# Two expert blocks of layer 0 moved into layer 1's opening list, a fourth early block in layer 1, and other PSUM banks for the first transposes

## The chip, the cores and the metric

The kernel runs on one core of a Trainium2 chip. The metric is the device time of one launch in microseconds (us). Before the change it is 1606.35 us, the median of three runs that lie between 1605.81 and 1606.99. The page of the profile shows one execution with a span of 1586.5 us, taken by the hardware profiler; the rest of a launch lies outside the span. In the page PE is TensorE's matmul, PEld its weight load, DVE is VectorE, ACT is ScalarE, POOL is GpSimd, and SP is SyncE, which here only starts transfers.

## The reference, cut to what matters

The input is x with N = 2708 rows of C = 256 floats, and an adjacency matrix of 2708 x 2708. Two layers follow each other. Each adds two terms to x:

```python
# layer 0
x = x + gnn0(layernorm(x), adj)      # softmax(leaky_relu(f1 + f2.T) + adj) @ h
x = x + ffn0(layernorm(x))           # causal attention with 4 heads, then 8 experts, 2 per row
# layer 1
x = x + gnn1(layernorm(x), adj)      # sigmoid(softmax(leaky_relu, masked by (adj != 0) | eye) @ Xp)
x = x + ffn1(layernorm(x))           # 8 experts, 2 per row, no attention
# the experts of a layer, flat = its normalised rows
for e in range(8):                   # weights: zero for all but the row's two best experts
    out += weights[:, e:e+1] * ((silu(flat @ w1[e].T) * (flat @ w3[e].T)) @ w2[e].T)
```

An expert's hidden width is 682. All matmuls that matter here are in float32. A row of layer 1's input x1 is complete only when both of its experts in layer 0 have added their share, and layer 1's graph attention mixes all rows.

## The kernel before

The 2708 rows are cut into NT = 22 tiles of 128 (the last holds 20). The kernel has four stages, and each is a stretch of the profile.

**`first`** is layer 0 up to its routing: the graph attention, the causal attention, and `route`, which picks two experts for each row and sends the row, with its gates and its index, by an indirect transfer (L1769) into the list of each of its experts in the DRAM buffer `xs[0]`. An expert's list is cut into NB = 6 blocks of 128 places, so a layer has 48 blocks. Within a list the rows stand in the order of their tiles. As soon as enough tiles have been sent (the `EARLY` numbers 12, 12, 18), the first three blocks of expert 0 are computed inside the same stage, by `early_blocks` (L514 to L582).

**`experts_blocks(0)`** is a plain loop over the other 45 blocks. For each it fetches the block's rows (`fetch`, `xt<-xs`), transposes them with two matmuls (L274) and copies them back on ACT (L276, L279), does 22 matmuls with w1 and w3 (`up`, L1981), the silu on ACT (L1985, L1988), the gate product on DVE (L1986, L1989), 6 matmuls with w2 (`down`, L1995), the row's weight on DVE (L1997) and an indirect scatter-add on POOL into `acc` in DRAM (`add_rows`, L598). Each float32 matmul shows as two records in the profile. Transposes and copies run ahead of the block that uses them. Three rooms hold the weights of three experts; `arena` is two of them, and expert 7's weights are in its second half, `arena[:, WE:]`.

**`second`** is layer 1 up to its routing. It loads x1, which is `acc`, from DRAM into `X` with five transfers (L1486, L1489). `prepare` makes of every tile its features: statistics on DVE (L257, L259, L1436), a power on POOL (L1440), the scaling on DVE (L1444), two transposes on PE (L1450) into a PSUM bank, a copy back on ACT (L1454), the matmuls with the layer's weights (L1459, L1462), and the results to `hb` and `sb` by DVE and ACT (L1466 to L1472). The 22 target tiles are taken in groups of six (four groups, the last with four tiles). For a group the mask of the adjacency, which `first` left in DRAM as bf16 (`mb`), is brought in by transposing transfers (L1504); for each source tile ACT makes the exponentials (L1511), DVE turns the mask to zeros and ones (L1516, L1520) and multiplies (L1522), and PE adds six products into six PSUM banks (L1529). Group 0's masks lie in `arena`, where layer 0's weights were, group 1's in a buffer of their own, and so on in turn. When a group is through, `finish` (L1575 to L1588) joins it to x, and `route` sends its rows into `xs[1]`. Three early blocks of expert 0 end this stage too.

**`experts_blocks(1)`** is the same loop over 45 blocks, with `out` in the place of `acc`.

The order within `first` and `second` is not written out by hand. `Plan` is a list scheduler that runs while the program is built. A step has an engine, a planned length, the steps it needs, the buffers it takes and gives back, a rank, and `lands`, the time until its transfer has landed. `issue` always takes the step that could start soonest in its planned time, the smaller rank first among those that can start together, and so fixes the order in which each engine meets its instructions. Every engine then works strictly in that order. Where the plan sees PE idle for over 1 us, `fill` puts matmuls named `nobody` there (L1248, L1630), whose results are not used; `issue(behind=5.0)` does so once more at the end of the list.

PSUM has eight banks. `second` uses six of them under the name `po` (the sums of a group, or the `up` results of an early block) and two under the name `mm` for everything else.

A flag is raised on the device if a block holds rows that its early place does not allow; if it is set, the whole network is computed again in a general form.

Of the kernel before, what the change touches and what calls it, by code (L numbers as in the profile page):

```python
# [39 lines left out]
EARLY = 12, 12, 18  # L40

CAP = (NT + 1) * P
# [99 lines left out]
def adj_ffn_kernel(ctx, tc, x, adj, vecs, bias_rows, tab, w_gnn0, w_gnn1, wqkv, wo,  # L142
# [216 lines left out]
    def route(add, tiles, ready, copied, cleared, layer, XB, xs, pool, turn_tile, turn_bank, gate_tile, gate_bank, rank):  # L359
# [151 lines left out]
        return [add("POOL", 2.3, lambda t=t: send(t), [b, c] + cleared, rank=rank + 6, lands=2.0) for t in tiles]  # L511


    def early_blocks(add, layer, needs, sent, we, xs, acc, new, named, rank):  # L514

        for k, before_t in enumerate(EARLY):
            v = {}
            names = dict(named, up=named["up"][k % len(named["up"])], xt=named["xt"][k % len(named["xt"])])

            def fetch(k=k, v=v):  # L520
                v["xt"] = new["xt"](k)
                after_all(nc.sync.dma_start(out=v["xt"], in_=xs[k * P:(k + 1) * P, :]), xs)
# [16 lines left out]
            def up(part, k=k, v=v):  # L539
# [28 lines left out]
            def down(half, v=v):  # L568
# [5 lines left out]
            def weigh(v=v):  # L574
                v["ys"] = new["ys"]()
                nc.vector.tensor_scalar(v["ys"], v["y"][:, :C], v["xt"][:, C + 1:C + 2], None, ALU.mult)
# [5 lines left out]
            a = add("SP", 0.4, fetch, (needs if layer == 0 else []) + sum([sent[t] for t in sent if t < before_t], []), take=[names["xt"]], rank=r, lands=3.0)  # L582
# [11 lines left out]
            add("POOL", 1.6, join, [a], give=[names["ys"], names["xt"]], rank=r)  # L594
# [174 lines left out]
    def first(X, XB, norms, tops, hd, mb, xs, acc, arena, load_weights):  # L769
# [11 lines left out]
        with ExitStack() as s:  # L781
# [449 lines left out]
            def chunks():  # L1231
# [4 lines left out]
                         weights_at(arena[:, :WE]), xs[0], acc,  # L1236
                         dict(xt=lambda k: (ab.tile([P, 2 * W2], F32, tag="osb", name="xt") if k == 2 else
                                            af.tile([P, NQK], F32, tag=("qk", "z")[k], name="xt"))[:, :ROW],
                              mm=mm_tile, xT=lambda: af.tile([P, KC, P], F32, tag="hT", name="xTs", bufs=3),
                              up=up_banks, sl=chunks, hT=chunks,  # L1240
                              ys=lambda: af.tile([P, C], F32, tag="xg", name="ys", bufs=3)),
                         dict(xt=["qk", "z", "ob"], mm="mm", xT="hT", up=[["st", "zs"], ["st", "o"], ["st", "o"]], sl="e", hT="e", ys="xg"), 60.0)
# [9 lines left out]
            with tc.manual_schedule():  # L1252
                plan.issue(behind=5.0)
# [143 lines left out]
    def second(X, XB, x1, x2, sd, mb, xs, arena, load_weights):  # L1397
# [9 lines left out]
        with ExitStack() as s:  # L1407
# [86 lines left out]
            def aggregate(g, tiles):  # L1494
# [72 lines left out]
                for i in tiles:  # L1567
                    finish(i, v, done, rank + NT + 2 + 3 * (i - tiles[0]), ["z"] * (i == tiles[-1]))
# [610 lines left out]
```

## Time and profile before

The table gives stretches of the profiled execution in us from the start of the span: their length, how long PE was busy in them (with the unused matmuls `nobody`), and the clock that was granted to TensorE.

| stretch | what runs there | length | PE busy | clock |
|---|---|---|---|---|
| whole span | | 1586.5 | 1483.3 | 0.97 |
| 600–700 | inside the loop of layer 0 | 100.0 | 100.0 | 1.00 |
| 525–531 | end of `first`, last early block | 6.0 | 6.0 | |
| 531–537 | `nobody`, then the loop's first transposes | 6.0 | 5.5 | |
| 885–891 | last block's end, then `nobody` | 6.0 | 5.8 | 1.00 |
| 891–899 | x1 is loaded | 8.0 | 0.0 | 0.62 |
| 899–906 | first tiles prepared | 7.0 | 5.7 | 0.70 |
| 906–916 | more tiles prepared | 10.0 | 8.9 | |
| 916–922.3 | wait for the first mask | 6.3 | 2.8 | |
| 922.3–963 | first group's products between the other tiles | 40.7 | 40.7 | 0.96 |
| 1183–1194 | after the last product: results joined, rows sent | 10.6 | 10.6 | |
| 1194–1203 | routing, early blocks | 9.0 | 6.8 | |
| 1203–1214 | early blocks | 11.0 | 11.0 | |
| 1214–1222.5 | `nobody`, then the loop's first rows | 8.5 | 6.0 | |

To read it: PE is busy for 93% of the span, DVE for 47%, ACT for 35% and POOL for 31%. Inside the expert loops PE has no gap. The stretches that are not full, or are full of `nobody`, lie at the seams between the four stages. A busy share counts `nobody` as work, so a seam is judged by what stands in it, not by its share.

### The profile page before, as it was taken

The numbers are of one execution on the slowest core, as the hardware profiler recorded it, in microseconds if no ns is written. First come the engines' busy times: TensorE is split into PE (matmuls) and PEld (weight loads), VectorE is DVE, ScalarE is ACT, GpSimd is POOL, SyncE is SP. The second block draws the span as 40 slices with busy tenths as digits, with TensorE's granted clock in tenths as the row PEclk, the third lists the DMA queues.
The fourth block names the chain that finished last, engine by engine and source line by source line (L and its number), as shares of the span: only waits on it lengthen the run. The fifth ranks groups of instructions, "written<-read, shape, count | busy, mean of one in ns | idle before, by whom it ended". The sixth has DMA issues, their size and how long they took to land. (4 is left out here: it accounts for less than half of the span.)

```text
span 1586.5 us, 23363 instructions
## 1 busy us (share of the span) xinstructions
PE 1483.3 (93%) x8998; PEld 1155.8 (73%) x8998; DVE 745.5 (47%) x1477; ACT 553.6 (35%) x1065; POOL 487.9 (31%) x680
## 2 busy tenths in 40 slices
PE   6888889889989999999999789999998999999996
PEld 5633433323335999999999678888768999999995
DVE  6798899955666122221111464766664221112221
ACT  3676676555544112111111263444332111111110
POOL 6665457462142222222211210030425122222121
PEclk9999899999999999999999899999999999999998
DMA  7688565440012233333222670524414333323111
GB/s 254 237 294 301 190 221 193 154 156 7 7 49 78 55 77 91 88 88 76 47 38 32 145 155 1 130 70 99 132 49 121 77 86 86 74 66 74 33 33 17
DMA packets 165998, 165.69 MB, mean 104 GB/s; under 512 B 81378, under 2 KB 145550, under 8 KB 163168
## 3 DMA queue, kind: packets, MB, share of 16 engines
q1 hardware_dynamic: 142582, 134.26, 28.0%
q0 software_dynamic: 19024, 26.24, 9.1%
q10 hardware_dynamic: 4270, 3.58, 0.7%
q8 instruction: 73, 1.20, 0.3%
q14 instruction: 49, 0.40, 0.1%
HBM read 87.38 MB, written 61.55 MB: 94 GB/s over the span
## 5 line engine op out<-in xcount | busy, mean ns | idle before, releaser
L1981 PEld LDWEIGHTS pup<-xTs,arena 128*128 128x128 f32 (+1 forms) x2904 | 332.9, 190 | 3.9 <-ACT xTs L279 0.7
L1981 PE MATMUL pup<-xTs,arena 128*128 128x128 f32 (+1 forms) x2904 | 335.0, 275 | 0.5 <-ACT xTs L279 0.5
L1986 DVE TENSOR_TENSOR hT<-sl,pup 128x640 f32<-128x640 f32 x90 | 73.9, 821 | 478.6 <-ACT sl L1985 478.6
L1985 ACT ACTIVATE sl<-pup 128x640 f32<-128x640 f32 x90 | 63.4, 704 | 520.3 <-PE pup L1981 510.1
L1529 PE MATMUL po<-hb,PT 128*128 128x257 f32 (+1 forms) x968 | 226.7, 388 | 2.9 <-DVE PT L1522 2.9
L1529 PEld LDWEIGHTS po<-hb,PT 128*128 128x128 f32 (+1 forms) x968 | 175.6, 188 | 43.1 <-issue 12.5
L1995 PE MATMUL y<-arena,hT 128*128 128x256 f32 x792 | 182.1, 380 | 0.6 <-DVE ys L1997 0.6
L1088 ACT ACTIVATE e<-stt 128x1024 f32<-128x1024 f32 (+1 forms) x132 | 126.6, 986 | 98.9 <-PE stt L1082 73.9
L1995 PEld LDWEIGHTS y<-arena,hT 128*128 128x128 f32 x792 | 145.3, 190 | 18.0 <-DVE ys L1997 1.0
L598 POOL DMA_INDIRECT acc<-ys,xt x48 | 74.9, 1559 | 247.1 <-DVE ys L1997 238.6
L598 POOL DMA_INDIRECT out<-ys,xt x48 | 74.7, 1557 | 245.0 <-DVE ys L1997 238.1
L1127 DVE TENSOR_TENSOR es<-es,e 128x1024 f32<-128x1024 f32 x104 | 125.8, 1210 | 38.4 <-ACT e L1088 31.7
L1082 PE MATMUL stt<-qT,kT 64*128 64x512 f32 (+1 forms) x528 | 134.3, 615 | 6.7 <-ACT e L1088 6.7
L1769 POOL DMA_INDIRECT xs<-XR,place x88 | 92.0, 1046 | 145.1 <-DVE mk L1516 40.2
L1108 PE MATMUL o<-e,V 128*64 128x512 f32 (+1 forms) x528 | 130.6, 618 | 1.6 <-ACT e L1088 1.2
L1981 PEld LDWEIGHTS pup<-xTs,room 128*128 128x128 f32 (+1 forms) x1056 | 121.2, 190 | 1.2
L1981 PE MATMUL pup<-xTs,room 128*128 128x128 f32 (+1 forms) x1056 | 121.9, 275 | 0.0
L1511 ACT ACTIVATE E<-sb,dcol 128x768 f32<-128x768 f32 (+1 forms) x88 | 75.2, 859 | 105.3 <-DVE PT L1522 105.0
L1082 PEld LDWEIGHTS stt<-qT,kT 64*128 64x128 f32 x528 | 44.1, 188 | 79.3 <-issue 61.0
L1108 PEld LDWEIGHTS o<-e,V 128*64 128x64 f32 x528 | 33.6, 141 | 77.0 <-issue 58.2
L1997 DVE TENSOR_SCALAR ys<-y,xt 128x256 f32<-128x256 f32 x90 | 43.5, 484 | 55.4 <-PE y L1995 55.4
L1995 PE MATMUL y<-room,hT 128*128 128x256 f32 x288 | 66.1, 379 | 0.0
(273 smaller groups left out, 1814.0 us busy)
## 6 DMA issues: line engine op xcount, KB each, us to landing
arena<-in_adj SPq DMA_DIRECT2D x21, 1354.0 KB, 7.5
arena<-in_w SPq DMA_DIRECT2D x36, 640.0 KB, 4.6
mb<-mb SPq DMA_DIRECT2D x44, 352.0 KB, 3.6
xs<-none SPq DMA_DIRECT2D x16, 804.0 KB, 8.0
xt<-xs SPq DMA_DIRECT2D x96, 134.0 KB, 2.1
room<-in_w SPq DMA_DIRECT2D x12, 640.0 KB, 4.5
acc<-X SPq DMA_DIRECT2D x21, 128.0 KB, 3.7
out<-X SPq DMA_DIRECT2D x21, 128.0 KB, 1.8
```

What stands on the lines that cost most here:

```text
L598: nc.gpsimd.indirect_dma_start(out=acc[:, :], out_offset=bass.IndirectOffsetOnAxis(ap=xt[:, C:C + 1].bitcast(I32), axis=0), in_=ys, in_off ...
L1082: nc.tensor.matmul(st[:r, g, c0(sb):], kT[a:b, sb * P:sb * P + r], qT[a:b, t0 + (sb == t0 + 1):t0 + 2, :, :], start=True, stop=True)
L1088: nc.scalar.activation(e[:r, :, c0(sb):], v[sb, "st"][:r, :, c0(sb):], AF.Exp, scale=1.0 / HD ** 0.5)
L1108: nc.tensor.matmul(v["o"][g * HD:(g + 1) * HD, c:], V[:r, sb, g * HD:(g + 1) * HD], v[sb][:r, g, c:], start=(n + i == 0), stop=(n + i == t ...
L1127: nc.vector.tensor_tensor(es, es, v[sb][:r, :, c:], ALU.add)
L1511: nc.scalar.activation(e[:q, :n], sb[:q, i0:i1], AF.Exp, bias=dcol[:q, j:j + 1], scale=SLOPE - 1.0)
L1529: nc.tensor.matmul(v["po", i][:r, :F], v["PT", j][:q, a:a + r], hb[:q, j, :], start=(j == 0), stop=(j == NT - 1))
L1769: i = nc.gpsimd.indirect_dma_start(out=xs[:, :], out_offset=bass.IndirectOffsetOnAxis(ap=at, axis=0), in_=src, in_offset=None)
L1981: nc.tensor.matmul(pp[:to, n, :], wn[:, c, :], xT[:, c, :], start=(c == 0), stop=(c == KC - 1))
L1985: nc.scalar.activation(sl, pp[:, :NF, :], AF.Silu)
L1986: nc.vector.tensor_tensor(hT[:, :NF, :], sl, pp[:, NF:2 * NF, :], ALU.mult)
L1995: nc.tensor.matmul(y, hT[:, n, :], w[3][:, n, :], start=(n == 0), stop=(n == NHC - 1))
```

## The change

The change works on the three seams.

- **Late blocks.** The last two blocks of layer 0, (7,4) and (7,5), leave the loop and become steps of `second`'s list (`LATE`). The tiles 0 to 11 of x1 are loaded before them, the tiles 12 to 21 after both have added their rows: a block this far back in its list holds rows of tiles from 12 on only, so the first load doesn't need it. `some_blocks` is the old `early_blocks`, made general to serve both; the blocks' rows are fetched into slots of `XR`, whose index column is written anew by an `iota` on POOL after the late blocks. Expert 7's weights are in the second half of `arena`, where the second half of group 0's masks will be. So these masks are now kept by tile (`by_tile`), three tiles of them are transposed in before the late blocks and three after, and the mask operations of group 0 take the new layout through rearranged views.
- **A fourth early block.** In layer 1 the block (1,0) is computed inside `second` as well, so that its loop has 44 blocks. The checks of the early and late blocks move to later places in the loops (`missed`, one flag for each block).
- **Other banks.** The first eight tiles' transposes of `prepare` take `po` banks, which are free until the first product, and leave the two `mm` banks to the matmuls behind them.
- **Planner.** `issue()` no longer puts matmuls at the list's end; planned lengths and lands are set anew (a send 2.7 instead of 2.3, a transpose 0.3, a product 0.44), and in the third group the joins stand 1 instead of 3 apart and routing begins at rank 8 instead of 14.

The aim is to have needed matmuls where PE now waits or does unused ones.

```diff
-EARLY = 12, 12, 18
+EARLY = ((0, 0, 12), (0, 1, 12), (0, 2, 18)), ((0, 0, 12), (0, 1, 12), (0, 2, 18), (1, 0, 12))
+LATE, LATE_T = ((7, 4), (7, 5)), 12
...
-        return [add("POOL", 2.3, lambda t=t: send(t), [b, c] + cleared, rank=rank + 6, lands=2.0) for t in tiles]
+        return [add("POOL", 2.7, lambda t=t: send(t), [b, c] + cleared, rank=rank + 6, lands=2.0) for t in tiles]
...
-    def early_blocks(add, layer, needs, sent, we, xs, acc, new, named, rank):
-        for k, before_t in enumerate(EARLY):
+    def some_blocks(add, layer, blocks, fetched, needs, weights, xs, acc, new, named, rank):
+        joins = []
+        for k, (e, j, before) in enumerate(blocks):
+            v = dict(xt=fetched[k])
+            we = weights(e)
...
+        return some_blocks(add, layer, blocks, [XR[:, k, :] for k in range(len(blocks))], needs, *rest)
...
-                plan.issue(behind=5.0)
+                plan.issue()
...
+                bank = "po" if t < 8 else "mm"
...
-                    v["pt"] = pt = psm.tile([P, 4, P], F32, tag="mm", name="pt")
+                    v["pt"] = pt = (pso if bank == "po" else psm).tile([P, 4, P], F32, tag=bank, name="pt")
...
-            loads, ends = [], (2, 7, 14, NT - 1)
+            loads, late, ends = [], [], (2, 7, LATE_T, NT - 1)
             for a, b in zip((0,) + ends, ends):
                 loads.append(add("SP", 0.45 * (b - a), lambda a=a, b=b: nc.sync.dma_start(
                     out=X[:, a:b, :], in_=x1[a * P:b * P, :].rearrange("(t p) c -> p t c", p=P)),
-                    rank=-9.0, lands=2.0 if a else 8.0))
+                    late, rank=-9.0, lands=2.0 if 0 < a < LATE_T else 7.0))
+                if b == LATE_T:
+                    late = some_blocks(add, 0, [(*b, []) for b in LATE], [XR[:, k, :] for k in range(len(LATE))], [],
+                                       lambda e: weights_at(arena[:, WE:]), xs0, x1, new, named, -20.0)
+                    for e in late:
+                        e["needs"] += loads
...
+            numbered = add("POOL", 0.3, lambda: nc.gpsimd.iota(
+                XR[:, :, C:C + 1].bitcast(I32), pattern=[[P, NT], [0, 1]], base=0, channel_multiplier=1), late, rank=-5.0)
...
-                got.append(add("SP", 2.8 * len(tiles), masks, take=[side[g]], rank=rank, lands=2.0))
+                if g == 0:
+                    a = add("SP", 2.8 * GI // 2, lambda: masks_by_tile(0), loads[:3], take=[side[g]], rank=-8.0, lands=2.0)
+                    got.append(add("SP", 2.8 * GI // 2, lambda: masks_by_tile(1), [a] + late, rank=-8.0, lands=2.0))
+                else:
+                    got.append(add("SP", 2.8 * len(tiles), masks, got[-1:], take=[side[g]], rank=rank, lands=2.0))
...
-                    m = v["mk"][:q, j, :n]
+                    m = by_tile[:q, :, j, :] if g == 0 else v["mk"][:q, j, :n]
...
-                    finish(i, v, done, rank + NT + 2 + 3 * (i - tiles[0]), ["z"] * (i == tiles[-1]))
+                    finish(i, v, done, rank + NT + 2 + (1 if g == 2 else 3) * (i - tiles[0]), ["z"] * (i == tiles[-1]))
...
-                    sent[t0] = route(add, range(t0, t0 + step), normed[t0:], [], [], 1, XB, xs, work,
+                    sent[t0] = route(add, range(t0, t0 + step), normed[t0:], [], [numbered], 1, XB, xs, work,
...
-                          g * NT + NT + 14 + t0 - tiles[0])
+                          g * NT + NT + (8 if g == 2 else 14) + t0 - tiles[0])
...
-                blocks = [(e, j) for e in range(NE) for j in range(NB)][len(EARLY):]
+                done = [b[:2] for b in EARLY[layer]] + list(() if layer else LATE)
+                blocks = [(e, j) for e in range(NE) for j in range(NB) if (e, j) not in done]
...
-                    if (e, j) == (1, 0):
+                    if (e, j) == (2, 0):
...
-                    if layer == 1 and (e, j) == (2, 0):
+                    if layer == 1 and (e, j) == (3, 0):
...
-                second(new_x(xp, 1), XB, acc[0], out, sd, mb, xs[1], arena, load_weights(1))
+                second(new_x(xp, 1), XB, xs[0], acc[0], out, sd, mb, xs[1], arena, load_weights(1))
```

## The prediction

> **What bounds the kernel now.** I read the busy totals first, then the windows by stage, then PE's own waits, then the timeline where these fall. Line numbers are those of the kernel before; where I say "order", I mean the order in which the built instructions of the changed kernel stand on each engine.
>
> ```profile
> PE 1483.3 (93%) x8998; PEld 1155.8 (73%) x8998; DVE 745.5 (47%) x1477; ACT 553.6 (35%) x1065; POOL 487.9 (31%) x680
> ...
> 600.00:700.00 100.00, 100.00 (x755) 95.97 (x754) 20.61 (x39) 19.46 (x52) 21.68 (x18) 1.00 0.39 92
> ...
> 891.00:899.00 8.00, 0.00 (x0) 0.00 (x1) 2.73 (x12) 0.00 (x0) 1.45 (x3) 0.62 0.81 261
> ```
>
> PE is the bound. In an expert stage it never pauses: a block has 44+12+4 = 60 matmul records, 755 records in 100 us make 12.58 blocks, **7.95 us a block**. The change keeps every block, so it can only win where PE does nothing needed: waits, and the fillers `nobody`, which the page counts as busy. Three such places lie in its reach.
>
> ```profile
> 528.10 2.76 PE L572 MATMUL pm<-arena,chunks 128*128 128x256 f32 x12
> 530.70 5.30 PE L1248 MATMUL nobody<-before,allones 128*128 128x128 f32 x46
> 535.83 0.38 PE L274 MATMUL pt<-ident,xt 128*128 128x128 f32 x2
> ...
> 885.49 5.30 PE L1630 MATMUL nobody<-before,allones 128*128 128x128 f32 x46
> 887.56 1.56 POOL L598 DMA_INDIRECT acc<-ys,xt  x1 [1.47 <-DMA acc<-ys,xt]
> 891.34 2.06 SPq L1486 DMA_DIRECT2D X<-acc  x4
> 895.62 22.62 SPq L1504 DMA_TRANSPOSE arena<-mb  x6
> 896.29 0.43 DVE L257 BATCH_NORM_STATS2 st<-X 128x6 f32<-128x256 f32 x1 [4.58 <-DMA X<-acc]
> 899.03 1.09 PE L1450 MATMUL pt<-ident,xn 128*128 128x128 f32 x4 [8.24 <-issue]
> ...
> 920.60 0.36 DVE L1516 TENSOR_SCALAR arena<-arena 128x768 bf16<-128x768 bf16 x1 [3.08 <-DMA arena<-mb]
> 922.34 2.53 PE L1529 MATMUL po<-hb,PT 128*128 128x257 f32 x8 [2.93 <-DVE PT L1522]
> ...
> 1214.07 5.30 PE L1630 MATMUL nobody<-before,allones 128*128 128x128 f32 x46
> 1221.27 0.41 PE L274 MATMUL pt<-ident,xt 128*128 128x128 f32 x2 [1.90 <-DMA xt<-xs]
> ```
>
> To be seen: at 530.7 only fillers stand between two needed matmuls. At 885.5 PE has finished layer 0; the last scatter must land before x1 is loaded, the load before the statistics, these before the first transposes at 899.0; then the first product waits for masks until 922.3. At 1214.1 PE waits for rows that the last scatters of layer 1's routing must bring.
>
> **The Trainium skill.** "PSUM — Partial Sum Buffer", Engine vs sequencer instructions: ACT, DVE and POOL are strict FIFO queues and matmuls start in program order. The trace fits: PE stood still at 922 behind one mask although later tiles could be prepared. "DMA: Bandwidth & Descriptors", Anatomy of one DMA: the fixed 2 us of a transfer is mostly the receipt of the last write. Here the scatter that left POOL at 889.12 freed the load at 891.34, 2.2 us on. "TensorE: Matmul & The Clock Gate", Part 1: after an idle window of about 3.4 us PE falls to half clock. Here the clock is 0.62 in 891–899 and 0.70 in 899–906, and four transposes take 1.09 us against 0.60 later.
>
> **Part a, no fillers at the lists' ends (`plan.issue()`).** Layer 0: the 46 records at 530.70 go, 535.83-530.70 = 5.1 us. The rows wanted next were requested at 524.37 and land in 2.1 us (xt<-xs), by 526.5, so nothing takes the fillers' place but a release of a PSUM bank of some 0.1–0.8 us. I take **5.0 us** (bounds 4.3 and 5.1). The other reordering inside layer 0's first list (rows go to XR, sends priced 2.7 instead of 2.3) I take as 0±2: the same steps in another order, beside attention matmuls that keep PE busy.
>
> **Part b, the two late blocks.** Let T be the end of the last block left in layer 0's loop. Before, two more blocks follow (15.9 us) and then 922.34-885.49 = 36.85 us to the first product: T+52.75. Until then 8 tiles were fully prepared and 9 transposed (records at L1459, L1450).
> After: the scatter, load and first statistics keep their distances, so x1's load issues at T+5.85, the statistics begin at T+10.8. In the order PE does 8 fillers (1.9), 4 transposes, then 22 and 16 of the up matmuls from about T+3.2 (5.1 and 3.7): T+12. Now a new wait. In DVE's order five tiles' statistics and three scalings stand ahead of the first block's gate product: 5×0.75+3×0.37 = 4.9 after T+10.8, with small waits T+16.3; the product's first part 0.7, so the down matmuls begin at T+17. PE idles some 4.5 us, long enough for the clock to drop: I add 1 us. Then down 2.65, six up 1.35, three tiles' transposes 0.65, four fillers 0.9, one tile 1.3, second down 2.65: T+27.5 with the 1 us. Weighting 0.5 with DVE work ahead 0.3, scatter 1.55, landing 2.2: x1's other tiles load from T+32. Behind this load three mask transposes queue on SP, and the first mask, so the first product, waits for them. Before, 2.77 MB of x1 and six transposes of 0.72 MB filled 891.34–920.60, 7.1 MB at 242 GB/s, with the DMA engines saturated; now 1.2+2.16 MB need 13.9 us: first mask at T+46, first product 1.74 later (922.34-920.60), **T+47.7**. Bounds: 3.15 us a transpose (median) with the load hidden, then 2.4 of landing (918.24 to 920.60) and 1.74, give T+45.6; 6.7 us (the longest of the trace) three times give T+57.
> By then the order has 10 tiles prepared and 12 transposed: 2×1.31+3×0.22 = 3.3 us of PE work less behind. Gain 52.75-47.7+3.3 = 8.3; 0.8 off for the fillers and waits that now stand among the remaining tiles: **7.5 us**. The by-tile mask layout costs nothing I can see: 353 ns a mask now; were it as slow as the float operation beside it (960 ns), DVE would need 2.15 us a step against PE's six products of 0.435 = 2.61. The new index ramp on POOL waits for the second scatter, about T+32; behind it queue the powers of the last twelve tiles, which PE reaches only after T+40, so it is hidden by the ten tiles ahead. The `po` banks for the first eight transposes relieve the two `mm` banks, worth the 2.9 us of waits on hb (PE's list of waits) at most; it is inside the count above.
>
> **Part c, the fourth early block and the tail.** From the last product (1183.42) I sum PE in the new order: two blocks' up matmuls 9.85; one transposed block 0.22, router transposes 2×0.44, logits 2×0.81, ranks 2×0.4: 3.5; four downs of 2.65 and two ups of 4.93: 20.5; ten fillers 2.3; waits for rT 1.0, for hot 0.4 (0.66 now) and for the last gate 0.6: 2.0. Together 38.1, to 1221.5; two transposes and the copy behind them (0.41+0.59) bring the loop's first up matmul to 1222.5, where it is now (1222.52), but one block ahead: 7.9 us. The rows wanted there come in time: the last sends can begin near 1208, four at 1.27, landing 2.7, fetch 2.1 gives 1218. Against it: the third group's results are now joined back to back, so DVE keeps the fourth group's masks waiting, and 8+5 fillers stand among its products instead of 4 (and 4 after them): 1 to 4 us, I take 1.9. **6.0 us** (3 to 8).
>
> Sum 5.0+7.5+6.0 = 18.5: 1606.35-18.5 = **1587.9 us**. Index checks moved to later blocks: one matmul more a layer, 0.13 us.
>
> **Rivals.** (1) *The masks give it back*: the second scatter lands in 3.8 us, the usual figure for acc, and transposes take nearer 6 us, first product near T+55. Part b is 52.75-55+3.3-0.8, about 0.3; with a 5 and c 6 the time is 1595. For: the DMA engines were saturated there; against: less is in flight. (2) *No bubble*: the gate product gets through early, PE is never idle, part b nears 15 and c 8: 1578.4. For: 885.49–962.97 is 77.5 us and holds 22×1.57 of preparation and 38 products of 0.435, so 26.5 us are lost there, far more than I recover. Against: the FIFO order above. (3) *Slower*: landing 3.8, the load alone 7.5, three transposes of 6.7, landing and mask 4.1: T+65.4, b -10; the starved fourth group takes c to 0, the reordered first list costs 2, a gives 4.3: -7.8, 1614. For: three transfers in series replace one burst, and SP keeps every later transfer queued behind them. Against: it needs every worst value at once.
>
> **Chances.** Forecast 0.57, rival 1 0.21, rival 2 0.16, rival 3 0.06. The forecast's own bounds (a 4.3–5.1, b 4–11, c 3–8) reach from 1582 to 1595; leaving out the slow rival and the outer half of the fast one, the range is 1576 to 1598. Faster by over 0.2% (3.2 us): all of the forecast and rival 2, 0.19 of rival 1: 0.92. Within: 0.02 of rival 1 and 0.01 of rival 3, 0.03. Slower: 0.05.
>
> **What would show it.** a: the first transposes of layer 0's loop follow the last down matmuls within 1 us. b: PE idle about 4.5 us before the first late down matmuls, waiting on the gate product; x1's second load near 32 us and the first product near 47.7 us after T. c: no wait for xt at layer 1's loop, which starts one block ahead. Wrong if the first product comes after T+52, or if the fourth group's products take over 4 us longer.

## The result, and the profile after

The changed kernel takes **1569.95 us** (median of four runs, 1566.79 to 1573.58) against 1606.39 for the kernel before: a ratio of 0.977 (95% interval 0.975 to 0.980), 36.4 us less. The forecast was 1587.9 with a range from 1576 to 1598: the sign is right, the size is half of what was measured, and the time lies below the range.

One thing has to be said before the profiles are compared. The kernel before does not take the same time on every chip: 1590 to 1592 us on three chips of this study, 1611 to 1612 on two others and 1606 in the first measurement, while the changed kernel took 1570 to 1574 on the two on which it ran again. (Each chip was used in one session only, so the runs can't tell the chip from the session.) The page of before that the prediction read took 1588.2 us, a time of the shorter kind. So two differences are to be explained: the 14.6 us between the two first pages, which is 21.4 us in the timed runs where before takes 1592, and some 15 us more that the first page of before does not hold.

The page of the changed kernel is one execution with a span of 1571.9 us:

```profile
PE 1479.6 (94%) x8926; PEld 1154.0 (73%) x8926; DVE 747.2 (48%) x1483; ACT 552.5 (35%) x1068; POOL 500.9 (32%) x684
```

PE is hardly less busy (1483.3 before): the time came out of waits and of `nobody` matmuls. Where, a table by stages shows best. Every number is a difference of two times in the timeline of PE (a stage begins with the start of its first matmul; the loop of layer 0 ends with the end of its last down matmul, the products with the end of the last product). E3, e7, e8, e11 and e18 are runs told of below.

| stage | before | before, e18 | after | after, e11 | e3 | e7 | e8 |
|---|---|---|---|---|---|---|---|
| first list, to the loop's first transposes | 535.8 | 537.4 | 525.9 | 522.6 | 520.7 | 520.1 | 528.8 |
| loop of layer 0 (45 or 43 blocks) | 349.8 | 349.8 | 334.6 | 334.6 | 349.8 | 334.6 | 334.6 |
| from there to the first product | 36.7 | 38.8 | 52.5 | 53.3 | 38.4 | 45.2 | 40.7 |
| the products | 261.2 | 274.1 | 261.4 | 259.8 | 255.0 | 259.1 | 260.4 |
| to the loop's first up matmul | 39.0 | 46.2 | 40.8 | 39.1 | 39.1 | 39.1 | 40.8 |
| rest (45 or 44 blocks) | 364.0 | 364.0 | 356.8 | 356.7 | 356.6 | 356.8 | 356.7 |

Down the columns "before" and "after": Some 10 us come from the first list, nothing from the seam between the layers (the loop, the way to the first product and the products take 647.7 before, 648.5 after), 5.5 from the tail and the fourth block. Pages of one kernel differ too, the first list by up to 4 us, so the single columns are rough. Now the seams one by one. At the end of layer 0's first list, PE's timeline after:

```profile
523.27 2.76 PE L578 MATMUL pm<-arena,chunks 128*128 128x256 f32 x12
525.86 0.38 PE L278 MATMUL pt<-ident,xt 128*128 128x128 f32 x2
```

The 46 `nobody` records are gone and the loop's first transposes follow the last down matmuls at once. But the last down matmuls begin at 523.27 instead of 528.10: 4.8 us were won earlier, inside the list.

At the seam between the layers (start, duration, and in brackets the idle time before and what ended it), PE:

```profile
860.32 1.95 PE L1664 MATMUL nobody<-before,allones 128*128 128x128 f32 x16
862.10 0.60 PE L533 MATMUL pt<-ident,XR 128*128 128x128 f32 x4
862.94 8.78 PE L555 MATMUL up<-xTs,arena 128*128 128x128 f32 x76 [0.24 <-ACT xTs L540]
...
877.73 4.64 PE L578 MATMUL pt<-arena,chunks 128*128 128x256 f32 x12 [6.00 <-DVE chunks L570]
...
891.57 2.09 PE L1475 MATMUL pn<-wg,xTs 128*128 128x258 f32 x4 [2.20 <-ACT hb L1488]
...
912.95 1.23 PE L1576 MATMUL po<-hb,PT 128*128 128x257 f32 x2 [2.95 <-DVE PT L1569]
```

The late blocks' up matmuls fill the time in which x1 is loaded, as meant. Then PE waits 6.0 us for the first late block's gate product, runs the twelve down records in 4.64 us instead of 2.75, and the first product starts at 912.95, 52.5 us after the loop's end at 860.5. DVE and the transfers started by SP, in the same stretch:

```profile
876.35 0.73 DVE L1460 TENSOR_SCALAR xn<-X,mv,prs 128x256 f32<-128x256 f32 x2
876.99 0.68 DVE L570 TENSOR_TENSOR chunks<-chunks,up 128x512 f32<-128x512 f32 x1
...
888.72 0.41 DVE L1460 TENSOR_SCALAR xn<-X,mv,prs 128x256 f32<-128x256 f32 x1 [2.66 <-DMA acc<-ys,XR]
...
891.58 0.47 DVE L582 TENSOR_SCALAR ys<-pt,XR 128x256 f32<-128x256 f32 x1
...
911.22 0.36 DVE L1563 TENSOR_SCALAR arena<-arena 128x768 bf16<-128x768 bf16 x1 [2.33 <-DMA arena<-mb]
```

```profile
868.54 13.04 SPq L1543 DMA_TRANSPOSE arena<-mb  x3
896.36 0.37 SPq L1513 DMA_DIRECT2D X<-acc  x1
...
897.42 11.39 SPq L1543 DMA_TRANSPOSE arena<-mb  x3
```

The gate product comes behind the statistics, at 876.99. The second late block's weighting (891.58) stands behind three tiles' statistics, and these behind a scaling that waits 2.66 us for a buffer `xn`, which the first block's result held until its scatter had landed. So the second scatter, and with it the second load on SP, comes late: between 881.6 and 896.4 SP issues no transfer, and three transposes still stand behind the load. At 911.22 DVE gets the first mask, for which the first product waits.

In the tail, PE:

```profile
1210.58 2.76 PE L578 MATMUL pt<-arena,chunks 128*128 128x256 f32 x12
1213.92 0.44 PE L278 MATMUL pt<-ident,xt 128*128 128x128 f32 x2 [0.58 <-DVE ys L582]
```

The wait for rows before the loop (1.90 us behind 46 `nobody` records) is gone, and one block more is done.

### The profile page after: what moved, and what is told of

The parts are those of the page before. It is cut to its first block, busy times and chain, and to the rows that moved or that the text cites. A ratio compares the mean times of both kernels' runs of the same rounds, so it can differ in the third digit from the quotient of the medians.

```text
span 1571.9 us, 23225 instructions
## 1 busy us (share of the span) xinstructions
PE 1479.6 (94%) x8926; PEld 1154.0 (73%) x8926; DVE 747.2 (48%) x1483; ACT 552.5 (35%) x1068; POOL 500.9 (32%) x684
## 5 line engine op out<-in xcount | busy, mean ns | idle before, releaser
L2015 PEld LDWEIGHTS pup<-xTs,arena 128*128 128x128 f32 x2772 | 317.8, 190 | 3.7 <-ACT xTs L283 0.7
L2015 PE MATMUL pup<-xTs,arena 128*128 128x128 f32 x2772 | 319.7, 275 | 0.5 <-ACT xTs L283 0.5
L1576 PE MATMUL po<-hb,PT 128*128 128x257 f32 (+2 forms) x968 | 226.0, 388 | 3.6 <-DVE PT L1569 3.6
L1576 PEld LDWEIGHTS po<-hb,PT 128*128 128x128 f32 (+2 forms) x968 | 176.1, 188 | 42.6 <-issue 11.9
L2029 PE MATMUL y<-arena,hT 128*128 128x256 f32 x756 | 173.8, 380 | 0.6 <-DVE ys L2031 0.6
L2029 PEld LDWEIGHTS y<-arena,hT 128*128 128x128 f32 x756 | 138.7, 190 | 17.3 <-DVE ys L2031 1.0
L1140 DVE TENSOR_TENSOR es<-es,e 128x1024 f32<-128x1024 f32 x104 | 130.6, 1256 | 31.2 <-ACT e L1101 24.5
L611 POOL DMA_INDIRECT out<-ys,xt x44 | 68.4, 1554 | 231.1 <-DVE ys L2031 221.9
L1803 POOL DMA_INDIRECT xs<-XR,place x88 | 95.2, 1081 | 135.0 <-DVE mk L1563 40.7
L611 POOL DMA_INDIRECT acc<-ys,xt x43 | 66.9, 1555 | 222.6 <-DVE ys L2031 221.1
```

The source lines that it names most:

```text
L611: nc.gpsimd.indirect_dma_start(out=acc[:, :], out_offset=bass.IndirectOffsetOnAxis(ap=xt[:, C:C + 1].bitcast(I32), axis=0), in_=ys, in_off ...
L1140: nc.vector.tensor_tensor(es, es, v[sb][:r, :, c:], ALU.add)
L1576: nc.tensor.matmul(v["po", i][:r, :F], v["PT", j][:q, a:a + r], hb[:q, j, :], start=(j == 0), stop=(j == NT - 1))
L1803: i = nc.gpsimd.indirect_dma_start(out=xs[:, :], out_offset=bass.IndirectOffsetOnAxis(ap=at, axis=0), in_=src, in_offset=None)
L2015: nc.tensor.matmul(pp[:to, n, :], wn[:, c, :], xT[:, c, :], start=(c == 0), stop=(c == KC - 1))
L2029: nc.tensor.matmul(y, hT[:, n, :], w[3][:, n, :], start=(n == 0), stop=(n == NHC - 1))
```

## The experiments

Each kernel was timed beside the kernel before on the same chip. E1 to e4 ran on one chip, e5 to e8 on a second, e9 to e12 on a third, e13 to e16 on a fourth, e17 and e18 on a fifth.

| run | kernel | time | before there | ratio (95% interval) |
|---|---|---|---|---|
| e1 | before | 1590.3 | 1589.6 | 0.999 (0.997–1.001) |
| e2 | before, no `nobody` at the lists' ends | 1587.6 | 1589.6 | 0.999 (0.997–1.000) |
| e3 | changed, late blocks back in the loop | 1565.1 | 1589.6 | 0.983 (0.980–0.987) |
| e4 | changed, three early blocks | 1574.6 | 1589.6 | 0.989 (0.986–0.993) |
| e5 | changed | 1573.5 | 1611.0 | 0.977 (0.975–0.979) |
| e6 | e2 with layer 0's sends planned at 2.7 | 1599.8 | 1611.0 | 0.993 (0.990–0.995) |
| e7 | changed, gate product ahead of statistics | 1563.8 | 1611.0 | 0.971 (0.970–0.973) |
| e8 | e7, masks ahead of the second load | 1557.7 | 1611.0 | 0.967 (0.965–0.969) |
| e9 | changed, old ranks | 1569.5 | 1591.7 | 0.986 (0.983–0.989) |
| e10 | changed, all transposes in `mm` | 1567.6 | 1591.7 | 0.984 (0.982–0.987) |
| e11 | changed | 1570.3 | 1591.7 | 0.986 (0.983–0.989) |
| e12 | before, one run for its page | 1592.2 | 1591.7 | |
| e13 | before, one run for its page | 1588.9 | 1590.7 | |
| e14 | before, new lengths in layer 1's list | 1598.7 | 1590.7 | 1.004 (1.003–1.006) |
| e15 | e4 again | 1574.8 | 1590.7 | 0.988 (0.986–0.990) |
| e16 | e9 again | 1569.9 | 1590.7 | 0.984 (0.982–0.987) |
| e17 | e8 again | 1558.3 | 1611.7 | 0.968 (0.966–0.970) |
| e18 | before, one run for its page | 1612.1 | 1611.7 | |

### The first list: e2 and e6

```diff
-                plan.issue(behind=5.0)        # e2: in both lists
+                plan.issue()
...
-        return [add("POOL", 2.3, lambda t=t: send(t), ...      # e6, besides
+        return [add("POOL", 2.7 if layer == 0 else 2.3, lambda t=t: send(t), ...
```

Expected of e2:

> The kernel before with issue() in the place of issue(behind=5.0) in both lists; nothing else. Prediction's part a: 5.0 us less in layer 0 (the first transposes of its loop right behind the last down matmuls), nothing in layer 1, where the rows are waited for anyway: 1601.4. Rival 1: the 18 us that the page of before does not show have to do with these matmuls, 1585 or less. Rival 2: rows arrive late in the timed runs, no change, 1606.

Expected of e6:

> The kernel of e2 (before, without the unused matmuls at the lists' ends) with the planned length of layer 0's sends 2.7 instead of 2.3; with it PE meets the instructions of layer 0's first list in exactly the order of the changed kernel. Theory: this number alone reorders the attention stage, and the order is worth 5 to 10 us (end of that list at 524 on the pages with the new order, 530 to 534 without): 1580 within 3, the loop's first transposes near 524. Prediction's step (other reordering 0 within 2): 1587.

E2's page shows the 5.1 us gone at the seam, but its timed runs gain only 2.0 (interval 0 to 4.5), and its first list ends at 534.2 where before has 533.6 to 537.4: PE came some 3 us later to the end of its wait at 515 (518.00 instead of 514.69) although the order is the same up to there. On the other pages with that order this point lies between 512.6 and 519.5, so one page can't resolve it; why the timed gain is below 5 is open. E6 changes one number of the plan besides, and the two together take 11.1 us off (8 to 16); its list ends at 523.6. With it PE meets layer 0's first list in the order of the changed kernel. What that order removes, PE's timeline shows, first the page of before, then e6:

```profile
458.43 1.99 PE L1082 MATMUL stt<-qT,kT 64*128 64x512 f32 x8
464.10 1.11 PE L398 MATMUL pm<-ident,XR 128*128 128x128 f32 x4 [3.68 <-ACT XR L392]
465.14 3.68 PE L1108 MATMUL o<-e,V 128*64 128x512 f32 x8
468.75 2.44 PE L1082 MATMUL stt<-qT,kT 64*128 64x512 f32 x8
```

```profile
458.60 1.99 PE L1082 MATMUL stt<-qT,kT 64*128 64x512 f32 x8
460.52 0.66 PE L398 MATMUL pm<-ident,XR 128*128 128x128 f32 x4
461.11 1.94 PE L1108 MATMUL o<-e,V 128*64 128x512 f32 x8
462.97 1.99 PE L1082 MATMUL stt<-qT,kT 64*128 64x512 f32 x8
```

In the old order PE comes to routing's transposes 3.7 us too early, and the matmuls after the wait run at half speed (3.68 us for eight records instead of 1.94). From the matmuls in front of the wait (458.43) to those behind (468.75) that is 10.3 us against 4.4. The wait stands in the first page of before, in those of e1 and e12 and in e2's, and not in e6's or the changed kernel's; in e1 the same stretch takes 9.8 us and in e2 9.2. So a longer planned send is worth 5 to 6 us on the page, and e6 against e2 some 9 us in the timed runs, though on another chip. E6's forecast end of the list, 524, came (523.6); its forecast time, 1580, had been set for a chip where before takes 1590.

### The late blocks: e3, e7, e8, e17

```diff
-LATE, LATE_T = ((7, 4), (7, 5)), 12                      # e3; its checks go too
+LATE, LATE_T = (), 12
...
-                    late, rank=-9.0, lands=2.0 if 0 < a < LATE_T else 7.0))     # e7, e8
+                    late, rank=-9.0, lands=10.0 if a < LATE_T else 7.0))
...
-            a = add("SP", 0.4, fetch, before, rank=r, lands=3.0)                # e8
+            a = add("SP", 0.4, fetch, before, rank=r, lands=3.0 if before else 0.0)
...
-                bank = "po" if t < 8 else "mm"                                  # e8
+                bank = "po" if t < LATE_T else "mm"
...
+                    late_down = some_blocks.down                                # e8: the last late down matmul
...
-                    got.append(add("SP", 2.8 * GI // 2, lambda: masks_by_tile(1), [a] + late, rank=-8.0, lands=2.0))
+                    got.append(add("SP", 2.8 * GI // 2, lambda: masks_by_tile(1), [late_down], rank=-8.0, lands=2.0))
```

Expected of e3:

> The changed kernel with layer 0's last two blocks back in its loop; the other parts of the change stay (masks by tile, load of tiles 0 to 11 and 12 to 20, banks, fourth early block, no fillers at the ends). Prediction: part b is worth 7.5 us, so 1577.5. Theory from the two pages (from the end of layer 0's first list to the last product the changed kernel takes 0.9 us longer than before): part b is worth nothing, 1570 within 2. Rival: the unexplained 18 us of the timed difference stand at this seam, 1588.

Expected of e7:

> The changed kernel with the planned landing of x1's first three loads at 10.0 instead of 7.0 and 2.0, so that DVE meets the first late block's gate product ahead of the tiles' statistics; the work is the same. Theory: the late blocks cost time because PE stands 6.0 us behind statistics on DVE, then runs at a lower clock, and the second scatter, the second load and the masks all come later by as much; without it the first product comes near 46 us after the loop's end instead of 52.6: 1563 to 1566. Rival: the transfers in series alone set the first product, 1569 to 1571.

Expected of e8:

> As e7, and: late rows planned as landed from the start, all twelve first tiles' transposes in po banks, and the second half of group 0's masks waits for the late blocks' last down matmul only and so stands on SP ahead of x1's second load (it needs arena's second half, not the scatters). Theory: SP and the DMA engines stand idle for some 16 us in the changed kernel (880 to 896) while the masks could come; with them first, the first product comes near 40 us after the loop's end and 12 tiles' products cover x1's second load: 1558 to 1562. Rival: tiles 12 to 21 come later by these transposes and PE waits for them instead: 1565 or more.

Expected of e17:

> e8 again, the version with the gate product ahead of the statistics and the masks ahead of x1's second load, to see that its gain does not hang on one chip: 1556 to 1560, whatever the kernel before takes beside it (32 us less than before where that takes 1590, 50 less where it takes 1610).

Without the late blocks the changed kernel is not slower but faster, and below all three expectations: 1565.1, 24.5 us under before, against 1570.3 and 21.4 for the changed kernel (e11) on a chip where before takes 2.1 us more. So the late blocks, as they stand, cost some 3 to 5 us; as the two ran on different chips and the intervals of their ratios overlap, the size is an estimate. E3's SP and PE timelines:

```profile
880.56 23.40 SPq L1543 DMA_TRANSPOSE arena<-mb  x6
```

```profile
883.94 0.69 PE L1466 MATMUL pt<-ident,xn 128*128 128x128 f32 x2 [8.24 <-DVE xn L1460]
...
908.96 2.77 PE L1576 MATMUL po<-hb,PT 128*128 128x257 f32 x12
```

PE idles as before while x1 is loaded, but the load and six transposes follow in one burst, and by the first product at 908.96, which comes without a wait, eleven tiles are prepared, where before had eight and the changed kernel ten. The products then take 255.0 us instead of 261.

E7 leaves the late blocks and changes only planned landings of loads, so that DVE meets the gate product ahead of the statistics: 9.7 us less than e5 on the same chip, first product after 45.2 us, where e5's page has 52.6. E8 also lets the second half of the masks in as soon as the last down matmul has freed its room, ahead of the second load; besides, it plans the late rows as landed from the start and gives four more tiles `po` banks, and these three edits were not timed apart:

```profile
872.15 23.95 SPq L1545 DMA_TRANSPOSE arena<-mb  x6
896.19 0.53 SPq L1514 DMA_DIRECT2D X<-acc  x1
```

```profile
873.48 2.76 PE L578 MATMUL pt<-arena,chunks 128*128 128x256 f32 x12
...
904.10 1.03 PE L1578 MATMUL po<-hb,PT 128*128 128x257 f32 x4
```

The six transposes stand together again, the first block's down matmuls come without a wait at full speed, and the first product comes 40.7 us after the loop. The time is 1557.7, 15.9 less than e5; e17 gives 1558.3 on another chip. This is the fastest version of the study; both its chips are of the kind where before takes 1611 to 1612, and on one of the other kind it did not run. Both runs shorten what they were to shorten, so the cost of the late blocks was the order on DVE and of the transfers on SP, not the work.

### The banks: e10

```diff
-                bank = "po" if t < 8 else "mm"
+                bank = "mm"
```

Expected:

> The changed kernel with all first transposes in the two mm banks, as before. Prediction: the po banks relieve these two, worth 2.9 us at most: 0 to 3 us slower than the changed kernel. Rival: with transposes and the following matmuls in the same two banks PE waits for copies on ACT at each of eight tiles (0.4 us each) while it must get ahead of the masks anyway, so nothing changes: the first product is set by the masks.

E10 is 2.7 us faster than e11 beside it; the intervals overlap. The `po` banks bring nothing here: the first product comes 52.4 us after the loop (53.3 in e11) and waits for the masks, as the rival said.

### The fourth early block and the ranks: e4, e15, e9, e16

```diff
-EARLY = ..., ((0, 0, 12), (0, 1, 12), (0, 2, 18), (1, 0, 12))      # e4, e15
+EARLY = ..., ((0, 0, 12), (0, 1, 12), (0, 2, 18))
...
-... rank + NT + 2 + (1 if g == 2 else 3) * (i - tiles[0]) ...        # e9, e16
+... rank + NT + 2 + 3 * (i - tiles[0]) ...
-... g * NT + NT + (8 if g == 2 else 14) + t0 - tiles[0]) ...
+... g * NT + NT + 14 + t0 - tiles[0]) ...
```

Expected of e4:

> The changed kernel with three early blocks in layer 1 as before, so that its loop has 45; all else stays. Prediction: part c is worth 6.0 us, and the pages agree (15.3 us earlier by one block of 7.95, less 9.1 that it had already at the last product: 6.2): 1576. Rival: rows for the loop would have come in time with the new routing order anyway, so that the fourth block only moves work: 1570 to 1572.

Expected of e15:

> e4 again: the changed kernel with three early blocks in layer 1. It took 15 us less than before on the first chip. Theory A (the order of the list removes the extra time): where before takes 1606 to 1611, it takes 1575 to 1580 all the same. Theory B (the fourth early block removes it): 1590 or more there.

Expected of e9:

> The changed kernel with the third group's joins 3 apart and its routing at rank 14 again, as in the kernel before (their ranks in the plan; the work is the same). On the second chip the page of e6 shows 20 us more than e2 after the first product: 10 among the products, 9 between the last product and the loop. Theory A: the new ranks are what removes them (e5, the changed kernel on that chip, has 3.6 and 0 of them); with the old ranks the time rises by 3 to 6 us, and by up to 18 on such a chip. Theory B: the ranks are worth nothing or cost the 1.9 us of starved masks that the prediction set against part c: no change or 2 us less than the changed kernel, and the 20 us left with the fourth early block or the order.

Expected of e16:

> e9 again: the changed kernel with the old ranks of the third group. Equal to the changed kernel where before takes 1592. Theory A (the ranks are not what removes the extra time): 1570 to 1575 whatever before takes. Theory B (they are): 1585 or more where before takes 1606 to 1611.

Without the fourth block the time is 1574.6 and 1574.8, 4.4 us more than e11, and relative to the kernels before beside them 5.5 to 6.3 more: as forecast. E4's page shows what the block hides:

```profile
1207.70 0.66 PE L278 MATMUL pt<-ident,xt 128*128 128x128 f32 x2 [6.70 <-DMA xt<-xs]
```

PE waits 6.7 us for the loop's first rows, and the fourth block fills that wait. The ranks are worth nothing that these runs can show (1569.5 and 1569.9 against 1570.3). On the pages they move time: with the old ranks the products take 256.7 and 257.0 us (258.2 and 259.8 in e10 and e11), and the way to the loop and the loop together 399.1 and 399.0 (396.3 and 395.9), where PE waits 2.3 us for the first rows and does the block behind them more slowly. Neither pair ran where before takes 1606 to 1612, so their second question stays unanswered.

### The planned lengths alone: e14

```diff
-                a = add("PE", 0.5, turn, [a], take=["mm"], give=["xn"], rank=rank)
+                a = add("PE", 0.3, turn, [a], take=["mm"], give=["xn"], rank=rank)
...
-                a = add("PE", 1.5, times, [a], take=["mm"], give=["xT"], rank=rank)
+                a = add("PE", 1.3, times, [a], take=["mm"], give=["xT"], rank=rank)
...
-                        last[i] = add("PE", 0.5, lambda j=j, i=i: product(j, i), [a, last.get(i)],
+                        last[i] = add("PE", 0.44, lambda j=j, i=i: product(j, i), [a, last.get(i)],
```

Expected:

> The kernel before with the changed kernel's planned lengths in layer 1's front alone (a transpose 0.3, the features 1.3, a product 0.44), which reorders that list; all else as before. Theory A: the order of that list by itself changes what is lost there; where the kernel before takes 1606 to 1611 this one takes 1595 or less, where it takes 1590 this one takes 1585 to 1590. Theory B: the order is worth nothing anywhere, same as before; then what removes the extra time is the fourth early block or the late blocks.

Both theories failed: with lengths nearer to the measured ones, the kernel before is 8.0 us slower by the medians (0.3 to 0.6%). On its page the products take 258.1, 3 less than before, and the way to the loop 49.3 instead of 39; its first list, to which nothing was done, ends at 540.6, which stays unexplained. PE in that tail:

```profile
1213.84 2.62 PE L1630 MATMUL nobody<-before,allones 128*128 128x128 f32 x22
...
1229.51 5.30 PE L1630 MATMUL nobody<-before,allones 128*128 128x128 f32 x46
```

The plan orders the three early blocks behind each other, sees gaps, and fills them with matmuls that nothing needs: 13.3 us of them in this tail, 6.4 in the first page of before.

### Where the kernel before loses 20 us more: e1, e5, e11, e12, e13, e18

These are the two kernels unchanged.

Expected of e1:

> The kernel before, unchanged. Its timed runs gave 1606.4 us, but the execution on its page took 1588.2, while the changed kernel's page (1573.6) lies among its timed runs (1566.8 to 1573.6). Theory A (two courses): the kernel before can run in two ways, near 1588 and near 1606, decided by when some transfer lands in layer 0's first list; then a profile taken again shows either 1588 or 1606 within 3 us, and in the second case the extra 18 us stand in PE waits before 530 us. Theory B (profiled and timed runs differ always): the page again shows about 1588 and the timed runs about 1606.

Expected of e5:

> The changed kernel as it is, beside the kernel before on the chip on which e1 to e4 ran. There the kernel before takes 1590 us, where its first four runs took 1606. Theory A: only the kernel before was longer in those four runs; the changed kernel again takes 1570 within 3, and the change is worth 20 us here. Theory B: whatever was longer then held both kernels; the changed kernel takes 1554 here.

Expected of e11:

> The changed kernel again, as the measure for the two runs beside it: 1570 to 1574.

Expected of e12:

> The kernel before, for its page. If the timed runs of before beside it are near 1606 to 1611, theory A says that its page has some 20 us more than the first page of before in the stages after layer 1's first product, with waits for nothing the profile shows on ACT and PE, as e6 has. Rival: they stand in layer 0. If the timed runs are near 1590, the page shows no such waits.

Expected of e13:

> The kernel before, for its page, on whatever chip this is. Theory A (as for e12): where its timed runs are near 1606 to 1611, the page has some 20 us more than the others after layer 1's first product: products over 270 us instead of 261 to 262, the way to the loop over 45 instead of 39. Rival: the difference stands in layer 0. Where the timed runs are near 1590, the stages are those of the other pages of before.

Expected of e18:

> The kernel before, for its page, as e12 and e13. Where its timed runs are near 1606 to 1611, theory A says products over 270 us and over 45 us to the loop, with waits on PE that nothing in the profile ends; the rival, that the difference stands in layer 0. Where they are near 1590, the stages are those of the other pages.

E1, e12 and e13 ran where before takes 1590 to 1592, and their pages have the stages of the first page of before to within some 2 us. So of e1's theories B fails, since page and timed runs agree, and A is right only in that there are two times: each chip showed one of them. E5 ran on another chip than its text supposes, one where before takes 1611; it took 1573.5, and the change is worth 37.4 us there. E18 ran where before takes 1611.7, and its page has the rest: layer 0 is the same to within 1.6 us, the products take 274.1 instead of 261.2, the tail 46.2 instead of 39.0, 20.1 us together. PE's waits from 880 to 1250 in e18 (what waited, for what: us in total, times, longest), the longest of those that e12 does not have:

```profile
PE up L549 <- issue: 4.6, 6, 1.2
PE po L1529 <- DVE z L1555: 3.5, 3, 1.8
...
PE pt L572 <- DVE chunks L564: 2.6, 1, 2.6
PE po L1529 <- issue: 2.5, 1, 2.5
```

"Issue" is time in which an engine waited for nothing that the profile shows. At the change from the third to the fourth group, ACT's, PE's and DVE's timelines of e18, then PE's and DVE's of e12:

```profile
1137.49 0.63 ACT L1511 ACTIVATE E<-sb,dcol 128x404 f32<-128x404 f32 x1 [1.57 <-DVE PT L1522]
1144.01 0.63 ACT L1511 ACTIVATE E<-sb,dcol 128x404 f32<-128x404 f32 x1 [5.88 <-issue]
```

```profile
1127.01 15.16 PE L1529 MATMUL po<-hb,PT 128*128 128x257 f32 x68
1144.72 2.10 PE L1529 MATMUL po<-hb,PT 128*128 128x257 f32 x4 [2.54 <-issue]
```

```profile
1136.88 0.58 DVE L1522 SCALAR_TENSOR_TENSOR PT<-E,mk 128x404 f32<-128x404 f32 x1 [1.44 <-issue]
...
1143.39 0.58 DVE L1522 SCALAR_TENSOR_TENSOR PT<-E,mk 128x404 f32<-128x404 f32 x1 [5.56 <-PE po L1529]
```

```profile
1119.76 26.95 PE L1529 MATMUL po<-hb,PT 128*128 128x257 f32 x108
```

```profile
1129.62 0.58 DVE L1522 SCALAR_TENSOR_TENSOR PT<-E,mk 128x404 f32<-128x404 f32 x1 [1.44 <-PE po L1529]
...
1132.22 0.58 DVE L1522 SCALAR_TENSOR_TENSOR PT<-E,mk 128x404 f32<-128x404 f32 x1 [1.65 <-PE po L1529]
```

Where e12 runs 108 product records in one go, e18 stops after 68. The exponential on ACT that follows a wait of 5.9 us is not where it begins: it starts 0.04 us after DVE's multiplication has ended (1143.39 + 0.58), just as the exponential at 1137.49 follows the multiplication at 1136.88. That multiplication's wait of 1.44 us is put down to "issue" in e18 and to PE in e12, so the label is no proof that all inputs were there. The late step is DVE's, which waited 5.56 us, put down to a product of PE, where e12 has 1.65. PE stops meanwhile and then works at a lower clock (0.75 from 1135 to 1152). E6, on another such chip, has the same two stages long (272.5 and 48.0) though it has layer 0's new order and no `nobody` at the ends; so neither of these two removes the loss. The changed kernel on that chip (e5) has 265.0 and 40.8: it keeps 3.6 of the 20 us against its first page, 6.8 against e11's, and 3.2 in the timed runs (1573.5 against 1570.3). Which part of layer 1's change does this was not found: e14, e15 and e16, made to tell it apart, ran on a chip where before takes 1590.7. What holds DVE and PE in these waits is open too.

## Why the prediction was wrong, point by point

- **The base: wrong.** Everything was read from a page of 1588.2 us and then taken off 1606.35. The page could not show the 18 us between the two, and the prediction did not ask where they were. E18 shows them, on another chip of the slower kind, in the products and the tail of layer 1, in the reach of the change, and the changed kernel keeps 3 to 7 of them; that the first measurement lost them in the same place is inferred, since it left no such page. This is the bulk of the miss: on the chip where before takes 1592 the change is worth 21.4 us.
- **Part a, fillers, 5.0 us: the seam right, the gain not shown.** The seam is closed to the tenth of a microsecond it was worked out to (5.1 on the page). The timed gain of e2 is smaller, 2.0 (0 to 4.5), and the remainder isn't explained.
- **"The other reordering inside layer 0's first list, 0±2": wrong.** It was called the same steps in another order beside attention matmuls that keep PE busy. PE was not kept busy: the page had a 3.68 us wait on ACT at 464 in it, with half speed behind, and the new order passes it by. Pages with the new order end the list at 524.1 in the mean of thirteen, pages of before at 535.9 in the mean of five: 11.8, of which 5.1 are the fillers by the seam, so 6.7. The timed runs give the same total (11.1 in e6) and divide it otherwise, 2.0 for e2's edit and 9.1 for the order, on two chips; so the division is not settled.
- **Part b, 7.5 us: wrong.** (T is again the end of the loop's last block, 860.5 on the page after.) The seam on the pages is worth nothing, and e3 puts the late blocks at a cost of 3 to 5 us. The steps held up to the bubble: gate product forecast at T+16.3, measured at 16.5; PE idle forecast at 4.5 us, measured 6.0; loss by the clock behind it forecast at 1 us, measured 1.9 (4.64 instead of 2.75). The last down matmuls ended at T+28.5 instead of 27.5. The term that failed was "weighting 0.5 with DVE work ahead 0.3": the weighting began 2.6 us after these matmuls, behind three tiles' statistics and the buffer `xn` that waited for the first scatter to land. The second load came at T+35.9 instead of 32. From it to the first mask 14.9 were needed (13.9 forecast) and from there to the product 1.73 (1.74). That gives T+52.5 instead of 47.7, past the mark of 52 that the prediction had set. The ten prepared tiles were there, but the 3.3 us less work behind went into `nobody` matmuls (3.4 us among the products instead of 1.2) and into a clock of 0.85 instead of 0.91 in the first 20 us of the products, an estimated 1.2 us (0.06 of 20). (The forecast's bound T+57 adds up to 56.2; nothing hangs on it.)
- **Rival 1** came nearest for part b (T+55, gain 0.3), for a reason it did not give: not the landing of the scatter as such, but what stood behind it on DVE.
- **Part c, 6.0 us: right.** Tail and rest together take 397.0 in the mean of three pages of the changed kernel (397.5, 397.5, 395.9) against 403.4 in the four pages of before that took 1588 to 1592: 6.4. The 1.9 us set against it for the fourth group's masks fit the products on the pages, which are 1 to 3 us shorter with the old ranks (e9, e16) than in e10 and e11; tail and loop give this back, so the timed runs show none of it.
- **The sum.** From the pages: 5.1 + 6.7 + 0 + 6.4 = 18.2, nearly the forecast 18.5, because 6.7 us that were not forecast took the place of 7.5 that did not come. The agreement is a coincidence, and only the stages show it. The timed runs e11 have 21.4, 3.2 more than this sum.

The Trainium skill, "TensorE: Matmul & The Clock Gate", Part 1, gives an idle window of about 3.4 us before the half clock. In these traces less was enough in places: after 2.20 us idle, at 891.57 on the changed kernel's page, four records of L1475 took 2.09 us instead of 1.04. It is no rule either, for in e7 a longer wait was not followed by half speed:

```profile
899.92 2.87 PE L1576 MATMUL po<-hb,PT 128*128 128x257 f32 x12 [3.34 <-DVE PT L1569]
```

The same twelve records take 2.77 us in e3 without a wait, and e7's granted clock is 1.00 from 895 to 905. The measurement decides: the length of a wait alone does not tell whether half speed follows, and a wait of 2 to 4 us on PE can cost more than itself.

## What to carry to other kernels

Before a change is taken off a measured time, the page's own time must be held against it: 18 us between the two were time that the page could not show. Work moved into a gap is worth the gap only if what it takes from the in-order engines is free there: here two blocks filled PE's gap and put their gate product behind statistics on DVE and a second load behind scatters on SP, and two planned times, one dependency and four more tiles' banks (e8) turned a cost of 3 to 5 us into a gain. In a list scheduler a planned length is a knob on the whole order: one number was worth 5 to 6 us on the page and some 9 in the timed runs, three others, nearer to the truth, cost 8, so such a number is measured by itself.

## What was not expected of the hardware

- The same kernel takes 1590 us on three chips and 1611 to 1612 on two others, the difference lying in two stages of together 300 us and in waits that the profile does not explain (5.6 us on DVE behind a product of PE, six on PE of up to 1.2).
- A wait of PE of 2.2 us was followed by half speed (2.09 us instead of 1.04, then 1.06 instead of 0.61), one of 3.68 us likewise, which cost 6.0 us in all; one of 3.34 us in e7 was followed by full speed.
